# Transposing normed activations with VectorE's 32x32 blocks in place of TensorE's 128x128 transposes, in a two-layer state-space, feed-forward, attention and expert kernel

## The chip, the cores and the metric

The kernel runs on one core of one Trainium2 chip. The metric is the device time of one execution in microseconds (us), as the median of several runs. A profile is one more execution, recorded by the hardware profiler. Engines are named as the profile names them: PE is TensorE's matmul, PEld its weight load, DVE is VectorE, ACT is ScalarE, POOL is GpSimd, and SP is SyncE, which here only issues transfers.

## The reference, cut to what matters

The data are 2 sequences of 512 tokens with 512 features, in float32. Four blocks follow one another, and each adds its layer-normed output to the residual stream `x`:

```
x = x + ln(state_space(ln(x)))      # selective scan, 1024 channels, 16 states
x = x + ln(gptq_ffn(ln(x)))         # 4-bit weights, 512 -> 1376 -> 512
x = x + ln(attention(ln(x)))        # attention within each token, 16 x 16
x = x + ln(experts(ln(x)))          # shared MLP 512 -> 1024 -> 512, and a latent path
```

`ln` is a layer norm over the 512 features. Every block begins with a matmul over the features, so the normed rows, which lie with tokens on partitions, are needed with features on partitions: each 128 x 512 tile of tokens has to be transposed into four 128 x 128 pieces of a tile `hT` (128 features x 4 chunks x 512 tokens).

## The kernel before

A sequence of 512 tokens is called a batch, b = 0 or 1, and is cut into TB = 4 tiles of 128 tokens. All the work lies in one program, in stages:

1. The state-space block of batch 0 is prepared, and then the scan runs over both batches. In that long stretch, up to 584 us, the order on PE, ACT, DVE and POOL is written out by hand (`pin()` ties each instruction to its predecessor). Feed-forward 0 runs beside the scan of batch 1. The transposes in this stretch (lines 583 and 784) have code of their own, outside the functions that the change touches.
2. The stage `p3`: the output projection of batch 1 (`po`, line 1133), the down projection of feed-forward 0 (`fo`, line 1155), the normed tiles for feed-forward 1 (`norm_tiles` with the name `f1_i`, into `hT_f1`), and the norm of feed-forward 0's output (`gptq_norm(0)`). The sums `wq` that attention needs are built by VectorE here too (line 354).
3. `attention(0)`, `gptq(1)`, `gptq_norm(1)`, `attention(1)`, `latent(0)`, `latent(1)`, in this order of tracing. Here, and in `p3`, the order on each engine is not written out: the framework's scheduler sets it from the order of tracing and from what depends on what, and so it interleaves attention(0) with gptq(1), and attention(1) with latent(0). The last down projection (`pd` of batch 1) is pinned again.

`attention(b)` calls `layer_T(b, "a")` first (normed tiles into `hT_a`), multiplies them with a small weight (`pqkv`, 128 x 48 per tile, line 1249), does the attention of each token with some ten VectorE instructions, adds the result to `x`, and calls `layer_T(b, "l")` for the experts (`hT_l`). `gptq(b)` has eleven column blocks: `fg` and `fu` (gate and up, lines 367 and 947), an activation by ScalarE, a product `it` by VectorE (line 1231), and two blocks later the down projection `fo`. `latent(b)` has `pfe` and `pup` (line 1302), the routing logits `plg` (line 1287), `pr` (line 1333) and `pd` (line 1365).

Buffers around the change: the rows `xn` in `p3` come from a pool of three buffers (`jrow`), those of attention and experts from two (`nrow`). The matmul banks `mm` are three, the output banks `o` four. The weights `wg`, `wu`, `wup` and others go through one pool of three buffers (`w4`), filled by SP. SP issues its transfers one after the other, and each waits for its buffer to be free. The expert weights `wdn` (eight transfers) and the rows `gam` and `bet` are loaded once; in SBUF their tiles lie where pools of the earlier stages lay, so that such a load waits for the last reader of what lay there.

A tile is normed and transposed in `norm_tiles`: VectorE's statistics, POOL's power for the reciprocal root (line 127), VectorE's minus mean (line 140), ScalarE's scale and shift into `xn` (`apply`, line 150), and then these lines:

```python
tp = bank(f"tp_{name}_{i}").rearrange("p (k t) -> p k t", k=KH)
for kc in range(KH):
    nc.tensor.transpose(tp[:, kc, :], xn[:, ts(kc, P)], ident)
nc.scalar.copy(dst[:, :, ts(i, P)], tp)
```

Of the kernel before, what the change touches and what calls it, by code (L numbers as in the profile page):

```python
# [16 lines left out]
DRAM = bass.MemoryType.DRAM  # L17

P = 128
B = 2  # L20
S = 512
H = 512
NT = B * S // P
TB = S // P
KH = H // P


D_IN = 1024
NCH = D_IN // P
N_ST = 16  # L30
# [9 lines left out]
PACK = 8  # L40
IC = [min(P, INTER - i * P) for i in range((INTER + P - 1) // P)]

# [7 lines left out]

PW = 2 * P
NP = (INTER + PW - 1) // PW
# [4 lines left out]
def tile_sandwich(  # L57
# [5 lines left out]
    nc = tc.nc  # L63

    def pool(scope, name, bufs=1, space=None):
        kw = {"space": space} if space is not None else {"reuse_waits": "tile"}
        return scope.enter_context(tc.tile_pool(name=name, bufs=bufs, **kw))
# [20 lines left out]
    ident = const.tile([P, P], F32, name="ident")  # L88
# [25 lines left out]
    def moments(srcs, name):  # L114

        mv = stat.tile([P, TB, 2], F32, tag="mv", name=f"mv_{name}")
        for i, s in enumerate(srcs):
            st = stat.tile([P, 6], F32, tag="st", name=f"st_{name}_{i}")
            nc.vector.bn_stats(st, s)
            nc.vector.bn_aggr(mv[:, i, :], st)  # L120
        return mv
# [23 lines left out]
    def scale_bias(mv, name, n=TB):  # L145
        rs = rstd(mv, name, n)
        return rs, minus_mean(mv, rs, name, n)

    def apply(dst, src, rs, nm, i):
        nc.scalar.activation(  # L150
            dst, src, AF.Identity, bias=nm[:, i : i + 1], scale=rs[:, i : i + 1]
        )

    def xs(b):
        return x[b * TB : (b + 1) * TB]

    def norm_tiles(b, idx, dst, bank, xnew, name, interleaved=False):

        n = len(idx)
        rs, nm = scale_bias(moments([xs(b)[i] for i in idx], name), name, n)  # L160
        for j, i in enumerate(idx):
            xn = xnew(f"xn_{name}_{i}")
            src, dst_ = xs(b)[i], xn
            if interleaved:
                src = src.rearrange("p (r k a) -> p r k a", k=KH, a=2)
                dst_ = xn.rearrange("p (k a r) -> p r k a", k=KH, a=2)
            apply(dst_, src, rs, nm, j)
            tp = bank(f"tp_{name}_{i}").rearrange("p (k t) -> p k t", k=KH)
            for kc in range(KH):
                nc.tensor.transpose(tp[:, kc, :], xn[:, ts(kc, P)], ident)  # L170
            nc.scalar.copy(dst[:, :, ts(i, P)], tp)  # L171

    def normed_T(b, dst, bank, xnew, name, **kw):
        norm_tiles(b, range(TB), dst, bank, xnew, name, **kw)

    scans, now = [], [0]
    pool_at = [-9]
# [180 lines left out]
    hTs, o16 = {}, {}  # L358
# [14 lines left out]
    def gptq_norm(b):  # L373

        mv = moments(o16[b], f"fo{b}")
        mv16 = stat.tile([P, TB, 2], F16, tag="mv16", name=f"mv16_{b}")
        nc.vector.tensor_copy(mv16, mv)
        ve = stat.tile([P, TB], F16, tag="ve16", name=f"ve16_{b}")
        nc.vector.tensor_scalar(ve, mv16[:, :, 1], 1.0013580322265625e-05, None, ALU.add)  # L379
        sd16 = stat.tile([P, TB], F16, tag="sd16", name=f"sd16_{b}")  # L380
        nc.gpsimd.tensor_tensor(sd16, ve, half, ALU.pow)  # L381
        rs = stat.tile([P, TB], F32, tag="rs", name=f"rs16_{b}")
        nc.vector.reciprocal(rs, sd16)
        for t, o in enumerate(o16[b]):
            nc.vector.tensor_scalar(o, o, mv16[:, t, 0:1], None, ALU.subtract)
            nc.vector.tensor_scalar(o, o, rs[:, t : t + 1], None, ALU.mult)
            nc.vector.tensor_add(xs(b)[t], xs(b)[t], o)
# [5 lines left out]
    def xT_tile(name):  # L393
        return xTp.tile([P, KH, S], F32, tag="xT", name=name)
# [27 lines left out]
    with ExitStack() as mamba:  # L422
# [15 lines left out]
        def jrow(name):  # L438
            return jp.tile([P, S], F32, tag="j", name=name)
# [4 lines left out]
        def mbank(name):  # L444
            return ps_m.tile([P, S], F32, tag="m", name=name)

        u = [[None] * NCH for _ in range(B)]
        g = [[None] * NCH for _ in range(B)]
        dtT, scr, xT = [], [], []
        for b in range(B):  # L450
            t_ = smp.tile([R_DT + 1, S], F32, tag=f"dtT{b}", name=f"dtT{b}")
# [3 lines left out]
        nc.gpsimd.dma_start(out=wx, in_=W_x)  # L455
        Bbs = [[None] * NGI for _ in range(B)]
        Cbs = [[None] * NGI for _ in range(B)]
        st = {}
# [100 lines left out]
        with ExitStack() as p1:  # L559
# [5 lines left out]
            def bank1(i, name):  # L565
                return mbank(name) if i % 2 else ps_1.tile([P, S], F32, tag="mm", name=name)
# [3 lines left out]
            for i in range(TB + 2):  # L570
# [4 lines left out]
                if 0 <= i - 1 < TB:  # L575
                    j = i - 1
                    rs = rn[j]
                    nm = minus_mean(mvs[j], rs, f"m0_{j}", 1)
                    xn = jrow(f"xn0_{j}")
                    apply(xn, x[j], rs, nm, 0)  # L580
                    tp = tps[j] = bank1(j, f"tp0_{j}").rearrange("p (k t) -> p k t", k=KH)
# [68 lines left out]
        with ExitStack() as p2:  # L650
# [41 lines left out]
            def bank_free():  # L692
                return len(turns) < 2 or turns[-2][1] is not None
# [4 lines left out]
            def bank(name):  # L698
                while not bank_free():
                    yield None  # L700
                turns.append([name, None])
                return mbank(name)
# [142 lines left out]
            def add_normed(b, i, src, o):  # L845

                name = f"mo{b}_{i}"
                mv = moments([src], name)
                yield 1
                rs = rstd(mv, name, 1)  # L850
                nm = minus_mean(mv, rs, name, 1, True)
                yield 4
                apply(o, src, rs, nm, 0)
                yield 2
                nc.gpsimd.tensor_add(xs(b)[i], xs(b)[i], o)
                yield 1
# [3 lines left out]
            def wo_pair(b, i, j):  # L860
                w = wst.tile([P, 2, H], F32, tag="w4", name=f"wo{b}_{i}_{j}")
                nc.sync.dma_start(out=w, in_=w_out[j])
                return w
# [208 lines left out]
            for s in range(NS + 3):  # L1072
                k, gi = divmod(s, NGI)
# [44 lines left out]
        with ExitStack() as p3:  # L1118
            dq = pool(p3, "dq2", 1)
            o16p = pool(p3, "o16p", 4)  # L1120
            ps_o = pool(p3, "p3o", 6, PSUM)

            def obank(name):
                return ps_o.tile([P, H], F32, tag="o", name=name)

            dqg = once(dq)
            po = [obank(f"po1_{i}") for i in range(TB)]
            for j in range(NCH // 2):
                w = wo_pair(1, 0, j)
                for e in range(2):  # L1130
                    c = 2 * j + e
                    for i in range(TB):
                        nc.tensor.matmul(  # L1133
                            po[i], g[1][c][:, ts(i, P)], w[:, e, :],
                            start=(c == 0), stop=(c == NCH - 1),
                        )
            for i in range(TB):
                o = jrow(f"o1_{i}")
                nc.scalar.copy(o, po[i])
                for _ in add_normed(1, i, o, o):  # L1140
                    pass
            for _ in dqg:
                pass
            fo = [obank(f"fo0_{t}") for t in range(TB)]
            for i, m in enumerate(IC):
                j, e = divmod(i, 2)
                if not e:
                    w = wst.tile([P, 2, H], F32, tag="w4", name=f"wd0_{j}")
                    n = len(IC[i : i + 2])
                    nc.sync.dma_start(  # L1150
                        out=w[:m, :n],
                        in_=wd_d[i * P : i * P + n * m].rearrange("(k p) h -> p k h", p=m),
                    )
                for t in range(TB):
                    nc.tensor.matmul(  # L1155
                        fo[t], its[i][:m, ts(t, P)], w[:m, e],
                        start=(i == 0), stop=(i == len(IC) - 1),
                    )
            hTs["f", 1] = xT_tile("hT_f1")
            for i in range(TB):  # L1160
                norm_tiles(1, [i], hTs["f", 1], mbank, jrow, f"f1_{i}", interleaved=True)
            o16[0] = []
            for t in range(TB):
                o = o16p.tile([P, H], F16, tag="o16", name=f"o16_0_{t}")
                nc.scalar.copy(o, fo[t])
                o16[0].append(o)
            gptq_norm(0)
# [35 lines left out]

    def layer_T(b, name, **kw):
        hTs[name, b] = hp.tile([P, KH, S], F32, tag="hT", name=f"hT_{name}{b}")
        normed_T(b, hTs[name, b], tbank, nrow, f"{name}{b}", **kw)


    def gptq(b):
# [227 lines left out]
```

## Time and profile before

| | |
|---|---|
| runs shown | 954.11 us median of 3 (953.85 to 956.48) |
| the profiled execution | 955.89 us, of which the recorded span is 954.1 us |
| busy in the span | PE 862.3, DVE 675.2, POOL 484.0, ACT 420.2 us |
| granted TensorE clock, mean | 0.959 |
| from 584 us on | PE carries nearly the whole chain of waits |
| the touched transposes (line 170) | 20 tiles, four PE transposes each, and 20 copies by ACT (line 171) |

The page of the profile divides the span into 40 slices of 23.9 us, with a digit for the busy tenths of each engine. The timeline lists the instructions of an engine in order of time; the brackets at the end of a line hold the time for which the engine stood idle before it, and what released it. Three things are to be read from it here: where PE stands idle before or after a transpose, how busy VectorE is at that place, and what SP has queued.

### The profile page before, as it was taken

Reading aid. Unit: us, or ns where it says so; the run is one execution under the profiler, and the core shown is the slowest. Engines: PE = TensorE matmul, PEld = TensorE weight load, DVE = VectorE, ACT = ScalarE, POOL = GpSimd, SP = SyncE. Lnnn points to the kernel's source line nnn. Section 1 sums busy time; section 2 is a strip of 40 time slices with the busy share of each in tenths; the row PEclk is TensorE's granted clock in tenths of the full one; section 3 lists DMA queues with packets and bytes.
Section 4 is the critical chain, followed back from the end, with each engine's and each line's share of the span. In section 5 each row is a group of like instructions: output and inputs, shape, how many; then the busy total and the mean of one; then the engine's idle time right before and its main releaser. Section 6 shows DMA issues by size and latency. Waiting matters only on the chain.

```text
span 954.1 us, 7148 instructions
## 1 busy us (share of the span) xinstructions
PE 862.3 (90%) x2184; PEld 386.6 (41%) x2184; DVE 675.2 (71%) x783; ACT 420.2 (44%) x631; POOL 484.0 (51%) x351
## 2 busy tenths in 40 slices
PE   6977989779989899579999999998999998999994
PEld 3532434333534434234433444444544444445441
DVE  4968999999999998999999995535610034534225
ACT  3335775656666655476655640125320014322122
POOL 5665796777877777876877884440000000011002
PEclk9978999898999989889999999999999999998997
DMA  6439211010002854300111103455223221200101
GB/s 182 163 124 387 69 37 38 30 37 31 22 23 83 297 187 152 89 0 0 45 44 45 30 9 124 150 159 198 58 64 89 58 89 45 66 12 30 48 0 44
DMA packets 43816, 80.08 MB, mean 84 GB/s; under 512 B 7774, under 2 KB 20937, under 8 KB 43778
## 3 DMA queue, kind: packets, MB, share of 16 engines
q1 hardware_dynamic: 41506, 73.64, 23.6%
q0 software_dynamic: 1984, 5.47, 1.6%
q10 hardware_dynamic: 288, 0.52, 0.2%
q8 instruction: 17, 0.28, 0.1%
q14 instruction: 21, 0.17, 0.1%
HBM read 68.37 MB, written 11.24 MB: 83 GB/s over the span
## 4 chain that ended last, share of the span: by engine, by line
PE 46%; DVE 28%; issue 11%; POOL 5%; DMA 2%; ACT 1%; SPq 0%; DVEq 0%; POOLq 0%; ACTq 0%
DVE bx L1022 11%; DVE bx L1018 8%; PE pd L1365 6%; PE py L1050 5%; PE pup L1302 5%; PE fo L1155 4%; PE fu L367 3%; PE fo L1218 3%; POOL bx L1028 3%; PE fg L367 3%; PE fu L947 3%; PE fg L947 3%; PE po L1133 3%; PE po L916 2%; DVE u L475 2%
## 5 line engine op out<-in xcount | busy, mean ns | idle before, releaser
L1028 POOL TENSOR_TENSOR bx<-bx,C 128x1024 f32<-128x1024 f32 x128 | 302.0, 2360 | 115.3 <-DVE bx L1022 90.7
L1022 DVE TENSOR_TENSOR_SCAN bx<-da,bx 128x1024 f32<-128x1024 f32 x128 | 291.6, 2279 | 0.1
L1050 PE MATMUL py<-bx,ident 128*128 128x512 f32 x480 | 238.1, 626 | 35.6 <-POOL bx L1028 32.3
L1002 ACT ACTIVATE da<-dt,A 128x511 f32<-128x511 f32 x256 | 176.3, 691 | 161.6 <-DVE bx L1022 155.7
L1018 DVE TENSOR_TENSOR bx<-du,B 128x1024 f32<-128x1024 f32 x128 | 154.4, 1206 | 9.0 <-DMA B<-scr 5.1
L1050 PEld LDWEIGHTS py<-bx,ident 128*128 128x128 f32 x480 | 91.5, 198 | 164.1 <-issue 93.1
L1231 DVE TENSOR_TENSOR it<-it,fu 128x512 f32<-128x512 f32 (+1 forms) x11 | 7.6, 688 | 72.3 <-PE fu L367 72.3
L1302 PE MATMUL pup<-hT_l,wup 128*128 128x512 f32 x128 | 57.5, 604 | 0.0
L381 POOL TENSOR_TENSOR sd<-ve,half 128x4 f16<-128x4 f16 x2 | 2.1, 1045 | 109.0 <-DVE ve L379 109.0
L709 PE MATMUL pg<-xT,w_g 128*128 128x512 f32 x120 | 57.1, 604 | 0.0
L1365 PE MATMUL pd<-wdn,hid 128*128 128x512 f32 x128 | 55.3, 592 | 0.0
L127 POOL TENSOR_TENSOR rs_lo<-ve_lo,mhalf 128x1 f32<-128x1 f32 x8 | 5.5, 684 | 78.0 <-DVE ve_lo L125 78.0
L947 PE MATMUL fg<-hT_f,wg 128*128 128x512 f32 (+1 forms) x88 | 42.1, 597 | 0.0
L475 DVE SCALAR_TENSOR_TENSOR u<-px,ch,u 128x511 f32<-128x511 f32 (+2 forms) x48 | 35.8, 746 | 7.0 <-ACT u L468 5.9
L367 PE MATMUL fg<-hT_f,wg 128*128 128x512 f32 (+1 forms) x88 | 40.2, 593 | 0.7 <-ACT hT_f L171 0.7
L947 PE MATMUL fu<-hT_f,wu 128*128 128x512 f32 (+1 forms) x88 | 40.7, 592 | 0.0
L367 PE MATMUL fu<-hT_f,wu 128*128 128x512 f32 (+1 forms) x88 | 39.8, 593 | 0.0
L1218 PE MATMUL fo<-wd,it 128*128 128x512 f32 (+1 forms) x88 | 39.6, 592 | 0.0
L1155 PE MATMUL fo<-wd,it 128*128 128x512 f32 (+1 forms) x88 | 38.0, 593 | 1.6 <-DMA wd<-wd_d 1.6
L1365 PEld LDWEIGHTS pd<-wdn,hid 128*128 128x128 f32 x128 | 24.2, 190 | 30.7 <-issue 30.1
L1302 PEld LDWEIGHTS pup<-hT_l,wup 128*128 128x128 f32 x128 | 24.5, 195 | 28.8 <-issue 28.8
L1230 ACT ACTIVATE it<-fg 128x512 f32<-128x512 f32 (+1 forms) x11 | 6.6, 597 | 65.7 <-PE fg L367 65.7
(224 smaller groups left out, 1161.4 us busy)
## 6 DMA issues: line engine op xcount, KB each, us to landing
wo<-in_W_outT SPq DMA_DIRECT2D x20, 512.0 KB
B<-scr SPq DMA_DIRECT2D x16, 512.0 KB
C<-scr SPq DMA_DIRECT2D x16, 512.0 KB
wg<-wgu_d SPq DMA_DIRECT2D x10, 512.0 KB
wu<-wgu_d SPq DMA_DIRECT2D x10, 512.0 KB
w_x<-in_W_in SPq DMA_DIRECT2D x8, 512.0 KB
wgu_d<-w_gu POOLq DMA_DIRECT2D x16, 256.0 KB, 2.3
w_g<-in_W_in SPq DMA_DIRECT2D x8, 512.0 KB
```

Of the source, the lines that this page charges most:

```text
L367: nc.tensor.matmul(ps[:m], w[:, kc, e * P : e * P + m], hT[:, kc, :], start=(kc == 0), stop=(kc == KH - 1),)
L709: nc.tensor.matmul(ps, w[:, k, ts(e, P)], xT[b][:, k, :], start=(k == 0), stop=(k == KH - 1))
L947: nc.tensor.matmul(ps[:m], wt[j][a][:, kc, e * P : e * P + m], hT[:, kc, :], start=(kc == 0), stop=(kc == KH - 1),)
L1002: nc.scalar.activation(das[s % 2][:, i, 1:], st["dt", b, c][:, 1:], AF.Exp, scale=A[:, c, n : n + 1])
L1018: nc.vector.tensor_mul(bx, st["du"].unsqueeze(1).to_broadcast([P, NG, S]), Bbs[b][gi])
L1022: nc.vector.tensor_tensor_scan(flat, das[s % 2].rearrange("p n t -> p (n t)"), flat, 0.0, ALU.mult, ALU.add)
L1028: nc.gpsimd.tensor_mul(bxs[s], bxs[s], Cbs[b][s % NGI])
L1050: nc.tensor.matmul(st["y"], ident, bx[:, i, :], start=False, stop=last)
L1155: nc.tensor.matmul(fo[t], its[i][:m, ts(t, P)], w[:m, e], start=(i == 0), stop=(i == len(IC) - 1),)
L1218: nc.tensor.matmul(fo[t], its[i][:m, ts(t, P)], w[:m], start=(i == 0), stop=(i == len(IC) - 1),)
L1302: nc.tensor.matmul(ps, w[:, kc, ts(e, P)], src[kc], start=(kc == 0), stop=(kc == KH - 1))
L1365: nc.tensor.matmul(pd, hid[kc][:, ts(i, P)], wdn[kc], start=(kc == 0), stop=(kc == INT // P - 1),)
```

## The change

`norm_tiles` no longer takes a PSUM bank. In place of the four PE transposes and the ACT copy of each tile, VectorE issues 16 transposes straight from `xn` to `hT`. Each reads 32 partitions (tokens) by 4 x 32 columns and writes 32 partitions (features) by 4 x 32 columns, one 32 x 32 block for each of the four chunks. The loop over `a` picks the 32 tokens, the inner loop over `q` the 32 features of each chunk; so the input stays on its 32 partitions for four instructions, while the output moves to other partitions at every one. The five calls that go through it are feed-forward 1 (`f1`), attention 0 and 1 (`a0`, `a1`), and experts 0 and 1 (`l0`, `l1`): 20 tiles, 320 VectorE instructions.

```diff
+Q = 32
...
-    def norm_tiles(b, idx, dst, bank, xnew, name, interleaved=False):
+    def norm_tiles(b, idx, dst, xnew, name, interleaved=False):
...
             apply(dst_, src, rs, nm, j)
-            tp = bank(f"tp_{name}_{i}").rearrange("p (k t) -> p k t", k=KH)
-            for kc in range(KH):
-                nc.tensor.transpose(tp[:, kc, :], xn[:, ts(kc, P)], ident)
-            nc.scalar.copy(dst[:, :, ts(i, P)], tp)
-
-    def normed_T(b, dst, bank, xnew, name, **kw):
-        norm_tiles(b, range(TB), dst, bank, xnew, name, **kw)
+
+            blocks = xn.rearrange("p (k q j) -> p k q j", k=KH, q=P // Q)
+            for a in range(P // Q):
+                for q in range(P // Q):
+                    nc.vector.transpose(
+                        dst[ts(q, Q), :, i * P + a * Q : i * P + (a + 1) * Q], blocks[ts(a, Q), :, q, :]
+                    )
+
+    def normed_T(b, dst, xnew, name, **kw):
+        norm_tiles(b, range(TB), dst, xnew, name, **kw)
...
-                norm_tiles(1, [i], hTs["f", 1], mbank, jrow, f"f1_{i}", interleaved=True)
+                norm_tiles(1, [i], hTs["f", 1], jrow, f"f1_{i}", interleaved=True)
...
-        normed_T(b, hTs[name, b], tbank, nrow, f"{name}{b}", **kw)
+        normed_T(b, hTs[name, b], nrow, f"{name}{b}", **kw)
```

The scheduler then orders the unpinned stages anew. In the changed program as it is built, the first difference on any engine stands at the `f1` tiles, after line 140's `nm` of the third tile. On SP, the loads of `wd` for batch 1 and the first three of `wdn` now stand ahead of `wg_0`; `wu_0` stands behind all eight `wdn` and `gam`, and `wg_1` behind `bet`. On VectorE the 16 transposes of a tile stand in one run, and the 64 of `a0`, `l0`, `a1` and `l1` stand together; those of `f1` are broken by four or five line-354 sums, and the fourth tile's norm stands behind the third tile's transposes. On PE, `pqkv` is split into its four tiles, with `fg`, `fu` or `pup` matmuls between them. `plg` of batch 0 moves from `pr` to between two `pup` groups.

## The prediction

> **What bounds the kernel now.** I read the page's busy shares and slices first, then the chain of waits, then PE's timeline around each transpose, then SP's and VectorE's.
>
> ```profile
> PE 862.3 (90%) x2184; PEld 386.6 (41%) x2184; DVE 675.2 (71%) x783; ACT 420.2 (44%) x631; POOL 484.0 (51%) x351
> ...
> PE   6977989779989899579999999998999998999994
> ...
> DVE  4968999999999998999999995535610034534225
> ```
>
> The first row is the page's sum, the others its slices: VectorE is full in the scan (slices 3 to 23), and from slice 25 on, where all of the change lies, PE is at 9 and VectorE at 0 to 6. There the chain of waits is PE almost throughout, so time is won or lost only where PE waits or issues. These are PE's lines around the transposes:
>
> ```profile
> 651.02 1.04 PE L170 MATMUL tp_f<-ident,xn_f 128*128 128x128 f32 x8
> 652.35 0.66 PE L170 MATMUL tp_f<-ident,xn_f 128*128 128x128 f32 x4 [0.29 <-ACT hT_f L171]
> 654.00 0.66 PE L170 MATMUL tp_f<-ident,xn_f 128*128 128x128 f32 x4 [0.99 <-ACT xn_f L150]
> 655.33 3.70 PE L367 MATMUL fg<-hT_f,wg 128*128 128x512 f32 x8 [0.68 <-ACT hT_f L171]
> 658.87 3.60 PE L367 MATMUL fu<-hT_f,wu 128*128 128x512 f32 x8
> 663.91 0.66 PE L170 MATMUL tp_a<-ident,xn_a 128*128 128x128 f32 x4 [1.45 <-ACT xn_a L150]
> ...
> 694.93 0.65 PE L170 MATMUL tp_l<-ident,xn_l 128*128 128x128 f32 x4 [2.11 <-ACT xn_l L150]
> ...
> 793.07 1.02 PE L170 MATMUL tp_a<-ident,xn_a 128*128 128x128 f32 x4 [2.50 <-ACT xn_a L150]
> ...
> 827.21 0.66 PE L170 MATMUL tp_l<-ident,xn_l 128*128 128x128 f32 x4 [0.99 <-ACT xn_l L150]
> ```
>
> To be seen: PE stands idle ahead of each group of transposes, since in its order they stand before matmuls that were ready. A tile's four transposes take 0.47 us of the chain. SP's loads around them, and VectorE where it changes partitions:
>
> ```profile
> 640.91 0.37 SPq L111 DMA_DIRECT2D wg<-wgu_d  x1
> 647.78 0.36 SPq L111 DMA_DIRECT2D wu<-wgu_d  x1
> ...
> 653.59 4.63 SPq L1324 DMA_DIRECT2D wdn<-in_down_w  x8
> ```
>
> ```profile
> 61.80 0.28 DVE L515 TENSOR_TENSOR nb<-psm,rr 128x128 f32<-128x128 f32 x1
> 64.36 0.68 DVE L529 COPY bc<-pt 32x512 f32<-32x512 f32 x1 [2.27 <-PE pt L524]
> 65.05 0.06 DVE L661 MEMSET da<- 128x2 f32 x2
> ```
>
> [...] the copy of partitions 32 to 63 at 64.36 ends at 65.04, and the next starts at 65.05; at 287.35 the same copy (0.683) ends at 288.03 and the scan starts at 288.06. Instructions that stay on their partitions overlap: line 1278's four of 0.69 take 2.50, that is 0.60 apart. [...] after the idle 2.50 at 790.6 the windows view shows a granted clock of 0.50 from 794 to 796, and the four records of `pup` at 794.10 take 3.04 instead of 1.72 (not so after the idle 2.11 at 692.8).
>
> **The price of one transpose, d.** Lower end if held: 0.28 (line 515) and 0.01 to 0.03 to the next, 0.29 to 0.31. [...] I take 0.32. If not held, 0.28 less the overlap of 0.69 - 0.60 = 0.09: 0.20. A second pass for four-byte elements would add 0.13 (VectorE's products take 1.22 for 1024 columns and 0.69 for 512, so 0.53 for 512 and 0.13 for 128): 0.45. So 320 instructions add 102 us to VectorE, in a stretch where it is mostly idle; what matters is the 20 us of a group of 64 against PE's next need.
>
> **Removed.** 20 x 0.47 = 9.4 us of PE, the 20 ACT copies (0.59 each, hidden, except in the waits above), and the waits ahead of the transposes.
>
> **Feed-forward 1 (`f1`).** `xn` of the first tile is ready at 631.2; VectorE is free at 631.9, under `fo`, which ends at 651.3. Three tiles are 48 x 0.32 = 15.4, five line-354 sums between them 5 x 0.69 = 3.5: 650.7. Only then the fourth tile's norm: POOL's root and line 140 take 1.04 (631.90 to 632.94 before), `xn` 1.11, and 16 x 0.32 = 5.1: 658.0. So `fg` starts at 658.1 instead of 655.33. Cover gone: ACT's four casts of `fo`, queued behind that `xn`, go from 649 to 653, and `gptq_norm(0)` behind the transposes. Next, SP: the fifth `wdn` lies where the last `xn` lay, so it waits for the last transpose, and with it all behind: three more `wdn`, `gam`, then `wu_0`. Five of 256 KB and 512 KB are 1.84 MB; at the 390 GB/s of the windows 656 to 662, 4.7, and 2.3 before data flow (a 512 KB load issued at 609.48 let PE go at 613.15: 3.6, less 1.3 of data). `wu_0` lands at 658.0 + 7.0 = 665.0: `fu` starts 6.3 later than 658.7. `wg_0` is safe: its issue stands ahead, at 641.
>
> **Attention 0.** `fu`, `fg`, `fu` back to back end at 665.0 + 3 x 3.43 = 675.3. The `gptq_norm` chain: four statistics after 658.0 take 2.9, then the 10.45 from 652.57 to the `nm_a` end before, and one `it` product of 0.6: 671.9. First `xn` 672.8, then tiles at 5.1 each: 677.9, 683.0, 688.1, 693.2 (two `xn` buffers suffice, ACT needs 0.82). `pqkv` by tiles, 0.9 each, with two to four 0.86 matmuls between them, waits 2.7 + 1.7 + 1.6 + 0.8 = 6.8. The third block's `fg` comes at 696.0, against 686.65: **9.3 lost** up to here, with the transposes and the idle 1.45 already taken off.
>
> **Experts 0.** 64 transposes end about 736; the `it` product behind them is due for the bank of `fg_7` at 696 + 41 = 737: just covered. Won: 4 x 0.47 and the idle 2.11: **4.0**.
>
> **Attention 1.** `xn` at 793.0, tiles at 798.2, 803.3, 808.4, 813.5. PE has one `pup` group until 794.0, then waits 4.3 + 1.7 + 1.6 + 0.8 = 8.4 around `pqkv`. The fourth following `pup` half-group ends at 816.2, where the old order would have it at 804.69 + 2.75 x 3.43 = 814.1: **2.1 lost**.
>
> **Experts 1.** Won: 4 x 0.47 and the idle 0.99, **2.9**. The transposes end near 861; `pd` of batch 0 covers them until 864.5. The `lo` chain starts late behind them, so the eviction of `pfe` behind it on ACT comes near 881 instead of 876, 2.4 after the bank's next use if PE keeps its full clock there; before, the clock was 0.54 there, and `pfe` took 9.89 instead of 7.03. I count zero, -3 to +3. POOL has nothing late behind its one delayed root.
>
> **Clock.** Idle of 6.7 and 3.5 at `fg` and `fu`, and of 4.3 at `pqkv`, [...] **3.4 lost**, 0 to 5.
>
> **Sum.** -9.3 + 4.0 - 2.1 + 2.9 - 3.4 = 7.9 us slower. The profiled execution took 955.89 (span 954.1), 1.8 above the median of the runs; the difference is put on the median: 954.1 + 7.9 = 962.0.
>
> **Rivals.** (A) *Not held.* d = 0.20: `f1` is ready at 650.3, before `fo` ends; `wu_0` lands at 657.3; `pqkv` waits 0.8 and 2.4 only. The same steps give +4.3 + 4.0 + 3.8 + 2.9 = 15 won: 939. For it: VectorE is half idle, and nothing waits on data between the transposes. Against it: the copy at 287.35. It decides below d = 0.27. (B) *Gain and loss cancel.* d near 0.29 gives -5.5 + 4.0 - 0.2 + 2.9 = +1.2, less clock 0 to 3.4: 953 to 957. For it: row 515's 0.28. (C) *Four-byte elements take two passes,* d = 0.45: -26 - 10.5 + 6.9 - 3.4, and the `it` products late in experts 0: 987 or more. [...] (D) *The loads, not VectorE:* if `wdn` and `gam` were no obstacle, `fu` would follow `fg` at 661.5: 3.5 of the loss goes, 958.
>
> **How the numbers follow.** The held case, d 0.31 to 0.34, with its loads: 0.62, time 956 to 969 with the clock's bounds. A 0.15; B 0.16; C 0.07. A change under 0.3% (2.9 us) is about what a measurement of this kernel can't tell from none. Faster: A and a little of B, 0.18; same: most of B and the edge of the held case, 0.17; slower 0.65. The range from 948 to 973 takes in the held case, B and a part of the way to A; A's centre and C are left out.
>
> **What would show it.** Right: transposes 0.31 to 0.34 apart; PE idle some 7 us before `fg` near 651, with `fu` waiting for `wu`; `pqkv` four times waiting on VectorE; `wdn` on SP waiting for VectorE. Wrong: transposes 0.20 apart and `fg` at 651, or PE without waits in 651 to 700.

## The result, and the profile after

The kernel after takes 969.35 us (median of 4 runs, 966.97 to 971.39), the kernel before in the same comparison 954.78 us (953.85 to 956.48). The ratio is 1.0144, with a 95% interval from 1.0119 to 1.0169: slower, inside the range of the prediction, 7.35 us above its number. The profiled execution of after took 971.39 us with a span of 968.4, so its span stands 14.3 above that of before. One execution of the kernel with the experts alone, shown further down, took 1286.25 us at a granted clock of 0.65, and is left out of that kernel's time.

The page's sum of busy times, and the slices of PE and VectorE, answer to the first lines of before:

```profile
PE 860.7 (89%) x2104; PEld 382.9 (40%) x2104; DVE 769.4 (79%) x1103; ACT 409.5 (42%) x611; POOL 483.5 (50%) x351
...
PE   6968979878989799579999999986899997998994
...
DVE  5959998999999998999999975486976048686225
```

VectorE has 94.2 us more of busy time (769.4 - 675.2) and 320 instructions more. PE lost 80 instructions and only 1.6 us of busy time, though 9.4 us of transposes are gone: matmuls took longer where the granted clock was low, among other places from 658.5 to 664 (0.60) and from 667.5 to 673 (0.50). PE's timeline shows where (start, duration, then in brackets the idle time before and its releaser):

```profile
657.93 6.17 PE L371 MATMUL fg<-hT_f,wg 128*128 128x512 f32 x8 [5.39 <-issue]
667.18 6.67 PE L371 MATMUL fu<-hT_f,wu 128*128 128x512 f32 x8 [3.08 <-DMA wu<-wgu_d]
...
682.28 1.09 PE L1253 MATMUL pqkv<-w,hT_a 128*128 128x48 f32 x8 [1.56 <-DVE hT_a L173]
...
697.51 1.09 PE L1253 MATMUL pqkv<-w,hT_a 128*128 128x48 f32 x8 [0.48 <-DVE hT_a L173]
...
807.62 1.92 PE L1253 MATMUL pqkv<-w,hT_a 128*128 128x48 f32 x8 [4.23 <-DVE hT_a L173]
...
895.48 25.77 PE L1306 MATMUL pup<-hT_l,wup 128*128 128x512 f32 x56 [2.71 <-ACT exo L1316]
```

The first eight matmuls of `fg` and of `fu` take 6.17 and 6.67 instead of 3.70 and 3.60 after their idle times. For `fg` the view names no releaser; it starts 0.1 after the last transpose of `hT_f` has ended. `pqkv` now waits for VectorE's `hT_a` where it followed TensorE's own transposes before. The last line is a wait that before did not have, for ScalarE's eviction `exo`; there the 64 `pup` ran on without a gap:

```profile
879.25 27.63 PE L1302 MATMUL pup<-hT_l,wup 128*128 128x512 f32 x64
```

SP's timeline, and VectorE's, for the first of these:

```profile
643.15 16.49 SPq L1328 DMA_DIRECT2D wdn<-in_down_w  x5
...
660.21 0.38 SPq L112 DMA_DIRECT2D wu<-wgu_d  x1
```

```profile
641.48 8.84 DVE L173 STREAM_TRANSPOSE hT_f<-xn_f 32x128 f32<-32x128 f32 x28
...
652.78 5.04 DVE L173 STREAM_TRANSPOSE hT_f<-xn_f 32x128 f32<-32x128 f32 x16 [1.39 <-ACT xn_f L151]
...
673.96 0.69 DVE L1235 TENSOR_TENSOR it<-it,fu 128x512 f32<-128x512 f32 x1 [4.25 <-PE fu L371]
...
677.17 20.28 DVE L173 STREAM_TRANSPOSE hT_a<-xn_a 32x128 f32<-32x128 f32 x64 [0.88 <-ACT xn_a L151]
```

Sixty-four transposes take 20.28: 0.317 from one to the next. One lasts 0.303 (median), so each begins only when the one before it has ended; this is what the prediction calls held. That it comes from the partitions on which a transpose begins was the author's assumption there, and the runs below test it. The load of `wu_0` is issued at 660.21, behind five `wdn`: the first of them went at 643.15, the other four only from 657.89 on, when feed-forward 1's last transpose had ended. And `it`, which waits 4.25 for the late `fu`, stands ahead of attention 0's transposes.

How far after lies behind before at six points of PE's timeline (span times; the blocks are counted from 0, so the third one is that of `fg_3`):

| | before | after | behind |
|---|---|---|---|
| third block's `fg` | 686.65 | 700.23 | 13.6 |
| `pfe`, batch 0 | 780.11 | 789.49 | 9.4 |
| `pd`, batch 0 | 837.93 | 847.91 | 10.0 |
| `plg`, batch 1 | 865.45 | 875.38 | 9.9 |
| `pr`, batch 1 | 906.72 | 921.09 | 14.4 |
| end of the span | 954.1 | 968.4 | 14.3 |

So 13.6 is lost up to the third block, most of it at feed-forward 1 and attention 0, 4.2 won back in experts 0, 0.6 lost from there to `pd`, and 4.4 lost between `plg` and `pr` of batch 1. ScalarE's timeline shows the last:

```profile
876.09 0.81 ACT L151 ACTIVATE lo<-lo,nm_lo,rs_lo 128x512 f32<-128x512 f32 x1 [12.61 <-POOL nm_lo L135]
...
894.14 0.81 ACT L151 ACTIVATE lo<-lo,nm_lo,rs_lo 128x512 f32<-128x512 f32 x1
894.86 1.05 ACT L1316 COPY exo<-pfe 128x512 f32<-128x512 f32 x2
```

The norms `lo` of batch 0 pass in turn through VectorE, POOL and ScalarE. Before, they began at 848 under `pd`:

```profile
847.97 0.81 ACT L150 ACTIVATE lo<-lo,nm_lo,rs_lo 128x512 f32<-128x512 f32 x1 [8.41 <-POOL nm_lo L134]
...
876.02 0.59 ACT L1312 COPY exo<-pfe 128x512 f32<-128x512 f32 x1 [0.41 <-PE pfe L1302]
```

Now they stand on VectorE behind the 64 transposes of experts 1, begin on ScalarE at 876.09, and `exo` stands behind them (894.86 against 876.02 for its first copy before).

### The profile page after: what moved, and what is told of

It is laid out like the page before. It is cut to its first block, busy times and chain, and to the rows that moved or that the text cites. A ratio compares the mean times of both kernels' runs of the same rounds, so it can differ in the third digit from the quotient of the medians.

```text
span 968.4 us, 7288 instructions
## 1 busy us (share of the span) xinstructions
PE 860.7 (89%) x2104; PEld 382.9 (40%) x2104; DVE 769.4 (79%) x1103; ACT 409.5 (42%) x611; POOL 483.5 (50%) x351
## 4 chain that ended last, share of the span: by engine, by line
PE 36%; DVE 33%; issue 11%; POOL 10%; DMA 3%; ACT 2%; SPq 1%; POOLq 0%; DVEq 0%; ACTq 0%
DVE bx L1026 10%; PE py L1054 7%; DVE bx L1022 7%; POOL bx L1032 4%; PE pup L1306 4%; DVE hT_a L173 4%; PE fu L371 4%; PE fo L1222 3%; PE fu L951 3%; PE pd L1369 3%; PE fg L371 3%; PE fg L951 3%; PE po L920 2%; DVE hT_l L173 2%; DVE hT_f L173 2%
## 5 line engine op out<-in xcount | busy, mean ns | idle before, releaser
L1054 PE MATMUL py<-bx,ident 128*128 128x512 f32 x480 | 233.6, 616 | 38.4 <-POOL bx L1032 33.6
L1306 PE MATMUL pup<-hT_l,wup 128*128 128x512 f32 x128 | 61.8, 639 | 2.7 <-ACT exo L1316 2.7
L371 PE MATMUL fg<-hT_f,wg 128*128 128x512 f32 (+1 forms) x88 | 44.1, 647 | 5.4 <-issue 5.4
L371 PE MATMUL fu<-hT_f,wu 128*128 128x512 f32 (+1 forms) x88 | 42.9, 631 | 3.1 <-DMA wu<-wgu_d 3.1
L951 PE MATMUL fg<-hT_f,wg 128*128 128x512 f32 (+1 forms) x88 | 42.1, 597 | 0.0
L173 DVE STREAM_TRANSPOSE hT_a<-xn_a 32x128 f32<-32x128 f32 x128 | 38.7, 303 | 3.6 <-ACT xn_a L151 1.8
L173 DVE STREAM_TRANSPOSE hT_l<-xn_l 32x128 f32<-32x128 f32 x128 | 38.7, 303 | 3.1 <-ACT xn_l L151 1.3
L951 PE MATMUL fu<-hT_f,wu 128*128 128x512 f32 (+1 forms) x88 | 40.7, 592 | 0.0
L128 POOL TENSOR_TENSOR rs_ao<-ve_ao,mhalf 128x4 f32<-128x4 f32 x2 | 2.0, 1007 | 76.3 <-DVE ve_ao L126 76.3
```

What stands on the lines that cost most here:

```text
L173: nc.vector.transpose(dst[ts(q, Q), :, i * P + a * Q : i * P + (a + 1) * Q], blocks[ts(a, Q), :, q, :])
L371: nc.tensor.matmul(ps[:m], w[:, kc, e * P : e * P + m], hT[:, kc, :], start=(kc == 0), stop=(kc == KH - 1),)
L951: nc.tensor.matmul(ps[:m], wt[j][a][:, kc, e * P : e * P + m], hT[:, kc, :], start=(kc == 0), stop=(kc == KH - 1),)
L1054: nc.tensor.matmul(st["y"], ident, bx[:, i, :], start=False, stop=last)
L1306: nc.tensor.matmul(ps, w[:, kc, ts(e, P)], src[kc], start=(kc == 0), stop=(kc == KH - 1))
```

## The experiments

Each time stands against the kernel before on the same chip. "Ratio" is with its 95% interval. The scheduler is called the planner in the recorded expectations.

### What a transpose costs: which 32 partitions it begins on

**Output fixed.** The 320 transposes stay; four in a row write the same 32 partitions, those that they read. The values land in other places than the reference's.

```diff
-dst[ts(q, Q), :, i * P + a * Q : i * P + (a + 1) * Q]
+dst[ts(a, Q), :, i * P + q * Q : i * P + (q + 1) * Q]
```

> All 20 tiles through VectorE with the same 320 instructions and the same sizes and order, but the four with one input quarter write to one output quarter (partitions 32a) instead of to four; so the blocks land at wrong places and the values differ from the reference. Theory (held because the output's partitions change): three of four transposes follow 0.20 to 0.23 us after the one before, the fourth 0.315; 64 take some 15 us instead of 20, f1 is ready near 653, `fu` near 661, and 8 to 14 us of the 14.6 lost come back: 955 to 962 or less. Rival (0.315 is the instruction's own cost): the spacing stays at 0.315 and the time at 967 to 971.

Measured: 945.97 us, ratio 0.9893 (0.9867 to 0.9918). VectorE's timeline:

```profile
641.54 6.28 DVE L173 STREAM_TRANSPOSE hT_f<-xn_f 32x128 f32<-32x128 f32 x28
```

Twenty-eight take 6.28 instead of 8.84, 0.223 apart. So the same count of the same instructions is 1.1% faster than before, or 1.4% slower, by the partitions that they begin on. More came back than expected, all that was lost and 10 us more. The engines' order is that of after, so the scheduler's new order is not by itself the loss. The run does not say whether the output alone matters.

**Loops swapped.** Output fixed over four, input moving; the values are the kernel's own.

```diff
-for a in range(P // Q):
-    for q in range(P // Q):
+for q in range(P // Q):
+    for a in range(P // Q):
```

> Only the two loops around the block transposes change places: the output quarter q outside, the input quarter a inside, so that four transposes in a row write the same 32 partitions while each reads other ones. Same 320 instructions, same order of everything else. Theory (what is held is the output: a transpose waits for the one before it only where it writes to another partition quarter): spacing about 0.22 us, as where the output quarter was kept for four before, and the time comes out as there, 943 to 950 us. Rival 1 (what made that kernel fast was that each block stayed in its own quarter, input and output the same): spacing 0.316 us and 966 to 972 us. Rival 2 (a switch of the input quarter costs as much as one of the output quarter): spacing near 0.32 too, no gain.

Measured: 967.57 us, ratio 1.0117 (1.0072 to 1.0161). The same row of VectorE:

```profile
641.44 8.86 DVE L173 STREAM_TRANSPOSE hT_f<-xn_f 32x128 f32<-32x128 f32 x28
```

Nothing is won: the theory that only the output is held falls. Two explanations were left, a change of the input's partitions, or reading one quarter and writing another.

**Kept, but crossed.** Four in a row read quarter a and write quarter a + 1.

```diff
-dst[ts(q, Q), :, i * P + a * Q : i * P + (a + 1) * Q]
+dst[ts((a + 1) % 4, Q), :, i * P + q * Q : i * P + (q + 1) * Q]
```

> Open after the swap of the two loops: does a transpose wait where either of its two quarters changes from the one before (theory), or where it reads one quarter and writes another (rival)? The fast kernel had both: quarters kept over four, and input quarter equal to output quarter. Here they are kept over four and differ: four transposes in a row read quarter a and write quarter a+1. The output's values differ from the reference's. Theory: spacing 0.22 us on average and 944 to 949 us, as where input and output quarter were the same. Rival: spacing 0.316 us and 964 to 972 us, as in the kernel after.

Measured in one run: 944.49 us (before 955.02). All instructions on one tile:

```profile
L173 DVE STREAM_TRANSPOSE hT_a<-xn_a x128: 258/261/305, 669.3 to 803.6; 32x128 f32<-32x128 f32 x128
```

The median duration is 261 ns instead of 303 (260 with the output fixed, where 64 take 14.40 instead of 20.28), and the time is that of the kernel with the output fixed, 944.49 against 945.97. So crossing cost nothing that shows; a change of quarter from one instruction to the next does, in the output (0.317 in after) or in the input (0.316 with the loops swapped). The runs put a price on it: if 0.22 is the mean of one changed and three unchanged, and 0.317 a changed one, an unchanged one is by estimate 0.19 and the change costs 0.126 us. A tile has 16 pairs of quarters, and with one transpose for each pair a tile by itself can't keep both.

### The late load

**Ten loads on another queue.** `wdn`, `gam` and `bet` are issued by GpSimd; the order of PE's and VectorE's instructions is that of after.

```diff
-nc.sync.dma_start(out=t_, in_=down_w[ts(kc, P), :])
+nc.gpsimd.dma_start(out=t_, in_=down_w[ts(kc, P), :])
...
-nc.sync.dma_start(out=gam, in_=ln_gamma.partition_broadcast(P))
-nc.sync.dma_start(out=bet, in_=ln_beta.partition_broadcast(P))
+nc.gpsimd.dma_start(out=gam, in_=ln_gamma.partition_broadcast(P))
+nc.gpsimd.dma_start(out=bet, in_=ln_beta.partition_broadcast(P))
```

> The kernel after with one thing moved: the ten loads of wdn, gam and bet (256 KB each) are issued from GpSimd's queue instead of SyncE's, so that the load of wu_0 no longer stands behind loads that wait for feed-forward 1's last transposes. PE's and VectorE's instructions keep their order. Theory: the late wu_0 costs through VectorE: fu_0 late, hence its it product late, which stands ahead of attention 0's statistics and transposes and idled VectorE 4.25 us. Without it fu_0 follows fg_0 with no wait, VectorE's idle goes below 1 us, the third block's fg starts near 696 instead of 700.2, and the time is 963 to 966 us, 3 to 6 below the kernel after: what the prediction's sum had. Rival 1 (attention 0's transposes would have been as late anyway, or GpSimd's issues delay its power for the norm of feed-forward 0): 968 to 971 us. Rival 2 (the load queue is the main loss): below 958 us.

Measured: 967.06 us, ratio 1.0112 (1.0088 to 1.0136). PE's timeline, then VectorE's:

```profile
664.74 3.60 PE L371 MATMUL fu<-hT_f,wu 128*128 128x512 f32 x8
...
696.93 3.60 PE L371 MATMUL fg<-hT_f,wg 128*128 128x512 f32 x8
...
890.53 26.83 PE L1306 MATMUL pup<-hT_l,wup 128*128 128x512 f32 x56 [4.40 <-ACT exo L1316]
```

```profile
670.70 0.66 DVE L1235 TENSOR_TENSOR it<-it,fu 128x512 f32<-128x512 f32 x1
...
673.89 20.27 DVE L173 STREAM_TRANSPOSE hT_a<-xn_a 32x128 f32<-32x128 f32 x64 [0.88 <-ACT xn_a L151]
```

In the stage it did what was expected: no wait at `fu` and 3.60 for its first eight matmuls instead of 6.67, no idle time ahead of `it`, attention 0's transposes 3.3 earlier, the third block at 696.93 instead of 700.23. The time is 1 us above what was expected. It lies 11.1 above before where that of after lies 14.6 above, but the intervals of the two ratios overlap. In the profiles PE is 5.0 ahead of after at `pd` of batch 0, and 1.1 of that is gone at `pr` of batch 1: it waits for `exo` 4.40 instead of 2.71.

**Both edits.** The swap of the loops and the other queue.

> Both edits together: output quarter outside, and the ten loads on GpSimd's queue. Theory: the two losses are in series on VectorE's way to attention 0, so the gains add up to a few us each: the wait of fu_0 for wu (5.7 us where transposes were fast) goes, VectorE's 2.9 us idle ahead of attention 0 goes, and the time is 2 to 5 us below e5_swap, 940 to 945 us, faster than both kernels. Rival (with fast transposes PE itself sets the end from attention 0 on, and the wait for wu is made up there): within 1 us of e5_swap.

Measured: 966.62 us, ratio 1.0116 (1.0081 to 1.0151), since the swap had brought nothing. It adds one point to the wait for `exo`. PE's timeline here, then that of after:

```profile
877.50 7.11 PE L1306 MATMUL pfe<-hT_l,wfe 128*128 128x512 f32 x16
...
894.14 27.29 PE L1306 MATMUL pup<-hT_l,wup 128*128 128x512 f32 x56 [6.09 <-ACT exo L1316]
```

```profile
879.68 9.66 PE L1306 MATMUL pfe<-hT_l,wfe 128*128 128x512 f32 x16
```

With 7.11 for `pfe` the wait is 6.09; in after, with 9.66 at a granted clock of 0.73 (from 880 to 889), it was 2.71. From the start of `plg` to the end of the wait it is 20.1 in both, and in the two kernels with one edit: where PE is faster, it waits longer. In each kernel with the whole change PE goes on after `exo` the same time after experts 1's last transpose: 895.48 - 872.7 in after, 890.53 - 867.7 with the queue alone, 894.48 - 871.7 with the swap, 894.14 - 871.4 with both, all 22.8. With the output fixed it is 873.76 - 851.0, again 22.8, and there PE waits only 0.2. So the chain of norms behind the transposes sets the time of `exo` where they end late. It was not tried to take `exo` out from behind that chain.

### One part at a time

In these the parts that are not named have TensorE's transposes and ScalarE's copies, as before; the pattern is

```diff
+if name[0] not in "f":          # "a" attention, "l" experts
+    tp = bank(f"tp_{name}_{i}").rearrange("p (k t) -> p k t", k=KH)
+    for kc in range(KH):
+        nc.tensor.transpose(tp[:, kc, :], xn[:, ts(kc, P)], ident)
+    nc.scalar.copy(dst[:, :, ts(i, P)], tp)
+    continue
```

**Feed-forward 1 alone.**

> Only feed-forward 1's four tiles go through VectorE; attention's and experts' tiles go through TensorE and ScalarE as before. Theory (each VectorE transpose is held until the one before has ended, 0.315 us apart, and f1's 64 end after `fo`, with SP's `wu` queued behind them): `fg` starts near 658 and `fu` near 667 as after the change, so about 11 us are lost there; the attention chain then starts 8.6 us later than before, less than PE is late, so the idle 1.45 ahead of `tp_a` goes and about 8 to 10 us remain: 962 to 966. Rival (the loss is attention's, from `pqkv` waiting): within 3 us of before, 952 to 958.

Measured: 967.32 us, ratio 1.0106 (1.0072 to 1.0141); the profiled execution, the lowest of the four, has a span of 960.6. Its `fg` waits 5.24 and takes 6.52, its `fu` waits 2.04 for `wu` and takes 5.40: the losses of after at this place, with the transposes of attention and experts still on TensorE. Its third block begins at 692.81, 6.2 behind before, where after is 13.6 behind. The time is 1.3 above what was expected.

**Attention alone.**

> Only attention's eight tiles go through VectorE. Theory: no wait at `fg` and `fu`; `pqkv` waits 6 to 9 us in each attention against 3.3 (attention 0) and 5.7 (attention 1) that the transposes on TensorE and their idle time cost: some 3 to 8 us lost, 957 to 963. Rival (f1 carries all of the loss): within 3 us of before, 952 to 957.

Measured: 976.19 us, ratio 1.0205 (1.0176 to 1.0235), slower than the whole change, and 13 above what was expected. Up to `pr` of batch 0, PE lost 3.9 (828.22 against 824.34). The rest goes with the scheduler's order: in this kernel it puts TensorE's transposes for experts 1, both `plg` and a part of `pfe` ahead of `pd`, and the normed tiles of experts 1, which come after attention 1, are late. PE's timeline:

```profile
840.57 1.12 PE L173 MATMUL tp_l<-ident,xn_l 128*128 128x128 f32 x4 [5.32 <-ACT xn_l L151]
...
847.73 6.99 PE L1297 MATMUL plg<-wgt,hT_l 128*128 128x8 f32 x32 [0.68 <-ACT hT_l L174]
```

From 840 to 866 the granted clock is 0.50, with PE busy for 22.73 of 26 us, and `plg` takes 6.99 where before it took 3.72. In after, `pd` stood there and covered the delay.

**Experts alone.**

> Only the experts' eight tiles go through VectorE. Theory: `gptq(1)` covers experts 0's 20 us (4.0 won) and `pd` covers experts 1's (2.9 won), but the `lo` chain behind the last 64 transposes makes `pfe`'s eviction late, which took 4 us at the end of the changed kernel: 4 to 7 us won without it and 1 to 3 with it, 948 to 954. Rival (20 us of VectorE is never covered): slower than before, 957 to 962.

Measured: 972.25 us, ratio 1.0161 (1.0131 to 1.0191), far from what was expected. The profile is that of one more execution:

> The kernel with only the experts' layer on VectorE once more, for its profile: it took 972 us where 948 to 954 was expected. Theory: the loss lies in the second half of batch 1, where the planner's new order puts evictions of pr on ScalarE behind normed tiles that wait for VectorE's transposes with two buffers; the profile then shows PE waiting there for ScalarE, 15 us or more in all, and a lower clock after it, with nothing lost before batch 1's attention. Rival: the loss is in batch 0's feed-forward blocks, where the transposes delay it products; then pfe_0 starts later than before's 780.1.

Measured in one run: 967.11 us, 11.2 above before on its chip. VectorE's timeline in experts 1, and PE's in experts 0 and 1:

```profile
833.69 20.26 DVE L179 STREAM_TRANSPOSE hT_l<-xn_l 32x128 f32<-32x128 f32 x64 [0.94 <-ACT xn_l L151]
853.96 0.69 DVE L1329 TENSOR_TENSOR hid<-hid 128x512 f32<-128x512 f32 x1
```

```profile
712.84 6.77 PE L377 MATMUL fu<-hT_f,wu 128*128 128x512 f32 x8 [5.11 <-DVE it L1241]
...
854.71 22.12 PE L1375 MATMUL pd<-wdn,hid 128*128 128x512 f32 x46 [9.26 <-DVE hid L1329]
```

PE waits for VectorE in both places, not for ScalarE: a product, or a square, that PE needs stands behind 20 us of transposes. Both explanations on record had a piece of it: the larger loss is in batch 1, but by VectorE's order, and there is one in batch 0 too.

### Fewer changes of quarter

**Wide transposes** for attention and experts: four normed tiles in one buffer, one transpose for each pair of quarters.

```diff
+blocks = xall.rearrange("p i (k q j) -> p k i q j", k=KH, q=P // Q)
+to = dst.rearrange("p k (i a j) -> p k i a j", i=TB, a=P // Q)
+for a in range(P // Q):
+    for q in range(P // Q):
+        nc.vector.transpose(to[ts(q, Q), :, :, a, :], blocks[ts(a, Q), :, :, q, :])
```

> Attention's and experts' four normed tiles go into one buffer of 128x2048, and one transpose of 32x512 takes the block of all four tiles: 16 instructions per layer instead of 64, so 16 changes of quarter instead of 64. Feed-forward 1 stays as in the kernel after. Theory (a change costs about 0.13 us, a 32x128 without one 0.19): 0.65 to 0.85 us each, 10.5 to 13.6 us per layer instead of 20.3; the products of q, k and v, which the planner puts behind 8.6 us of other matmuls, wait little in both attentions; the third block's fg comes near 695 instead of 700.2, the wait for exo goes, since the last transpose of experts 1 ends over 8 us earlier, and the time is 948 to 956 us. Rival 1 (all columns pay what a 32x128 of the kernel after pays, 1.26 us for a 32x512): no gain per layer and, with the overlap by tiles gone, 968 to 976 us. Rival 2 (feed-forward 1 alone costs the 14 us): 962 to 967 us.

Measured: 966.55 us, ratio 1.0134 (1.0105 to 1.0162). VectorE's timeline, then PE's:

```profile
804.49 11.45 DVE L187 STREAM_TRANSPOSE hT_a<-xn_a 32x512 f32<-32x512 f32 x16 [3.06 <-ACT xn_a L151]
```

```profile
665.72 5.37 PE L383 MATMUL fg<-hT_f,wg 128*128 128x512 f32 x8 [8.86 <-DMA wg<-wgu_d]
...
816.08 7.03 PE L1265 MATMUL pqkv<-w,hT_a 128*128 128x48 f32 x32 [4.17 <-DVE hT_a L187]
...
824.75 6.83 PE L1303 MATMUL plg<-wgt,hT_l 128*128 128x8 f32 x32
```

The price was right: 0.715 each, 11.45 a layer instead of 20.28. The time was not. The transposes wait 3.06 for four norms, `pqkv` waits as long as in after (4.17), now for all four tiles, and its 32 matmuls take 7.03 where before they took 3.77; `plg` behind them takes 6.83 where it took 3.72. And the scheduler put `wg_0` behind seven `wdn` on SP, so that now `fg` waits 8.86. The wait for `exo` is gone, as expected. The time lies where the second rival had it, with feed-forward 1 as the whole loss; the next run tests that.

**Wide, with feed-forward 1 on TensorE.**

> As the wide kernel, with feed-forward 1's four tiles on TensorE and ScalarE again, as before. Theory: what feed-forward 1 lost (late loads, half clock, late attention 0) is gone too; the third block's fg comes near 684.6 (before 686.65), attention 1 wins its 2.5 us wait and 1.9 us of transposes, experts 0 and 1 some 3 us each, no wait for exo over 1 us; 938 to 946 us, faster than the kernel before by 1 to 1.7%. Rival (the chain of last norms behind the transposes of experts 1 still delays exo, or the clock falls in new gaps): 950 to 956 us, no gain over the kernel before.

Measured: 960.23 us, ratio 1.0065 (1.0041 to 1.0089): 6.3 us better by feed-forward 1's part, but slower than before, so feed-forward 1 was not the whole loss. The time lies above both ranges on record. `pqkv` still waits, 3.03 and 4.16, and its 32 matmuls take 6.05 and 6.01 where before they took 3.75 and 3.77; the granted clock is 0.59 from 678 to 690 and 0.61 from 806 to 824.

**Wide, experts only.**

> Only the experts' layer on VectorE, as in the kernel that took 972 us where 948 to 954 was expected, but with the four tiles in one buffer and 16 transposes of 32x512. Theory on that miss: its 64 transposes held VectorE for 20.3 us in one piece, behind which stood the product it_3 (PE waited 5.1 us for it) in experts 0 and the square hid_3_1 (PE waited 9.3 us) in experts 1. With 11.45 us in one piece PE waits under 1 us for it and 1 to 3 us for hid_3_1; won are the 3.8 us of TensorE's transposes and the 3.1 us that it stood idle ahead of them: 946 to 953 us, faster than the kernel before. Rival (the layer's place in the order is the loss, not the length of the piece): the waits stay over 5 us in one of the two places and the time is 956 us or more.

Measured: 955.92 us, ratio 1.0008 (0.9987 to 1.0029): no difference from before, and some 15 us less than the same part with 64 transposes (some 11 less than its one later run). VectorE's timeline, then PE's:

```profile
831.90 11.45 DVE L193 STREAM_TRANSPOSE hT_l<-xn_l 32x512 f32<-32x512 f32 x16 [2.99 <-ACT xn_l L151]
```

```profile
844.13 22.32 PE L1387 MATMUL pd<-wdn,hid 128*128 128x512 f32 x48 [3.39 <-DVE hid L1341]
```

The wait for `it` is gone and that for `hid` is 3.39 instead of 9.26: the length of the piece in VectorE's queue was the loss. What was won, 4.2 in experts 0 and 1.6 up to `pd`, was given back at that wait and at the slower matmuls behind it (22.32 for 48 that take 20.7 at 27.63 for 64): 5.0 together. That is why 946 to 953 was not reached. No version with the kernel's own values was faster than before.

## Why the prediction was right, point by point

The direction, the mechanism and the range were right. The number was not much more than half: 7.9 lost was predicted, 14.6 measured. The range, 948 to 973, took in no change at all too, so that it held says little about the size.

- **Price of one transpose, 0.32, held.** Measured 0.317. The 0.32, and the 0.34 of the range, were the author's estimate: what the trace of before shows gives 0.29 to 0.31. Rivals A, not held, B, near 0.29, and C, two passes, fall. With the quarters kept the time falls to 945.97, in the direction of A's 939 (at 0.20). By estimate, a straight line through the two measured kernels, 0.317 at +1.44% and 0.22 at -1.07%, crosses zero at 0.26; the prediction had 0.27.
- **`f1` ready at 658.0, `fg` at 658.1.** 657.8 and 657.93. The 1.4 us by which `fo` ended late (652.5, before 651.2) was not in the working: the sums of line 358, delayed between transposes, delay SP's `wq` loads and with them two `wd`. It was hidden behind the wait of `fg`.
- **`wu_0` at 665.0.** The cause was right (`wdn` and `gam` ahead), the size not: it landed near 667.1. The 7.0 from the last transpose to the landing counted the transfers, but not SP's own issues: five of 0.33 to 0.42 and the gaps between them put the issue of `wu_0` at 660.21, 2.2 after 658.0, and from there to the landing it took 6.92.
- **Attention 0, 9.3 lost, and the clock there, 1.7.** The 1.7 is half of the 3.4 that the sum has for the clock, an estimate of the author's that no trace of before showed. Measured 13.6 against these 11.0. This is the first of two terms that were mis-sized. The prediction let attention 0's transposes start at 672.8, as if `it` cost only its 0.6: by its numbers `fu` was done at 668.4. But `it` waits for `fu`, and `fu` began 2.2 later than predicted and took 6.67 at a granted clock of 0.50, so they started at 677.17. That clock cost 3.1 at `fu` and not 1.7, and it belonged in this chain, not at the end of the sum. The run with the other queue shows it: without the late load they start at 673.89 and the third block is at 696.93, which is 0.9 from the predicted 696.0. From the first transpose to the third block it is 23.0 to 23.1 in both kernels, and 23.2 in the prediction.
- **Experts 0, 4.0 won.** 4.2.
- **Attention 1, 2.1 lost, 1.7 by its clock, and 2.9 won by experts 1's transposes: 0.9 lost.** The first wait was 4.23 against 4.3; up to `pd` 0.6 was lost. The sum came near with other terms in it: `pqkv` waited 4.9 in all and not 8.4, with PE at a granted clock of 0.50 from 807.7 to 809.5, and clock was lost behind `plg` instead, where 24 `pup` took 12.24, at 0.86 from 829 to 841 (with the output fixed 10.55).
- **`exo`, counted zero.** This is the second term. PE waited 2.71. That this is near the 2.4 that the prediction had worked out for full clock, and then left out of the sum, is luck: with `pfe` at 7.11 the wait is 6.09 (the run with both edits), and the low clock of `plg` and `pfe`, 0.78 from 875.4 to 880 and 0.73 from 880 to 889, hid the rest. So the chain of norms was 3.7 later than the prediction had it. The `pup` behind the wait took 25.77 where the same 56 without a long wait take 24.30 (output fixed), 1.5 more. Together with what else lies between `plg` and `pr` it is 4.4, above the bound of 3. The bound left out the clock behind the wait, 0.57 from 895.48 to 899.

The sum: 7.9 predicted, 14.4 measured to `pr`. The difference is 2.6 in attention 0, -0.2 and -0.3 in the next two, and 4.4 at `exo`. Rival D (the loads alone) gave the queue 3.5 of the loss; without the late load the third block came 3.3 earlier, and the time was some 3 us lower, within what the intervals can tell.

## What to carry to other kernels

An engine that is half idle is still no free place for work that comes in pieces of 20 us: here all that was queued behind the piece (a product, a chain of norms, a load that waits for a buffer) was late, and where PE needed the late item it waited, and behind the waits of 3.08 and 4.23 it ran at a granted clock of 0.50. Before moving transposes to VectorE, count its changes of the 32-partition quarter, in the input and in the output (by estimate 0.126 us for each transpose with one here), and see which product stands next in its queue. A part measured alone tells of the scheduler's order for that part as much as of the part: by means, the three parts alone cost 10, 20 and 15 us (the last 11 in its later run) where the whole cost 14.

## What the runs showed of the hardware

- A 32x128 float32 transpose on VectorE came 0.317 us after the last where the output's quarter changed each time (64 in 20.28, in after) and 0.316 where the input's did (28 in 8.86, loops swapped). With both kept over four, and the quarter written the one that is read, it was 0.223 to 0.225 on the mean (28 in 6.28, 64 in 14.40), with a median duration of 260 ns; where another quarter was written the median was 261 ns. From 0.317 and 0.22, one without a change takes by estimate 0.19. A 32x512 with a change took 0.715 (16 in 11.45).
- Some short waits were followed by a low granted clock on PE. In after, the clock was 0.50 from 667.5 to 673 behind an idle 3.08, and eight `fu` took 6.67 instead of 3.60; behind an idle 4.23 it was 0.50 from 807.7 to 809.5, and eight small `pqkv` took 1.92 instead of 0.99. Behind nearly the same wait it could be otherwise: the four `tp_a` of batch 1 took 1.02 after an idle 2.50 before, and 0.66 after an idle 2.43 with the wide experts alone. In the kernel with attention alone the clock was 0.50 from 840 to 866, through transposes with gaps of 0.7 and 64 matmuls of 8 columns, and 0.95 from 866 to 896, behind the start of `pd` at 864.96. What length of wait lowers the clock, and what brings it back, the runs don't show.
